# Spreading the dispatch of a soft mixture over its steps, and moving phi's fold and Mamba's weights into an expert stage

## The chip, the cores and the metric

The kernel runs on one core of one Trainium2 chip. The metric is device time in microseconds (us). Three runs of the kernel before took 2210.39, 2211.55 and 2219.65 us; the median is 2211.55.

## What is computed

Six residual layers over x of 4 x 1024 tokens of 128 features, in float32. Each layer reads a layer norm of x and adds its result to x. Cut to its core:

```python
x = x + 0.5 * moe(layernorm(x))       # "moe a": 8 experts, 2 of them for each token, hidden 512
x = x + mamba(layernorm(x))           # DI = 256, 16 states, convolution over 4 tokens
x = x + 0.5 * moe(layernorm(x))       # "moe b", the same weights
x = x + 0.5 * soft_moe(layernorm(x))  # "soft a": 64 experts x 32 slots
x = x + gla(layernorm(x))             # gated linear attention, 16 heads of 8
x = x + 0.5 * soft_moe(layernorm(x))  # "soft b", the same weights

def moe(x):        # cap = 1024 tokens for each expert
    top2 of softmax(x @ wg); a token takes the next free row of each of its two experts
    out = relu(rows @ w1[e] + b1[e]) @ w2[e] + b2[e]
    return gate0 * out[row0] + gate1 * out[row1]      # 0 where no row was free

def mamba(x):
    u, z = split(x @ W_in);  uc = silu(conv_b + conv4(u))
    dt, B, C = split(uc @ W_xproj);  delta = softplus(dt @ W_dt + b_dt)
    h[t] = exp(delta[t] * A) * h[t-1] + delta[t] * uc[t] * B[t]     # for 256 x 16 states
    return ((h . C + uc * D) * silu(z)) @ W_out

def soft_moe(x):
    logits = x @ phi_w.T + phi_b                       # (4096, 64 experts, 32 slots)
    rows = softmax(logits over slots).T @ x            # 2048 rows ("dispatch")
    y = tanh(layernorm(rows)) @ expert_w + expert_b
    return softmax(logits over experts) @ y            # "combine" of the soft layer
```

## The kernel before

**Layout.** x stays in on-chip memory as 32 tiles of 128 tokens (NT = 32). Nearly all work goes by groups of four tiles, 512 tokens. A layer norm of a group is: bn_stats and bn_aggr for each tile and "eps" (variance + 1e-5) on VectorE, one power of -0.5 on GpSimd (ln_pow), minus mean times that on VectorE (ln_minus), and then ScalarE applies scale and bias to a tile when it is needed (ln_apply, L201).

**Order.** In the main stretches (`with tc.manual_schedule(engines=ENGINES)`) TensorE, VectorE, ScalarE and GpSimd take their instructions in the order in which the program writes them. Each engine has one queue; an instruction waits for its data at the head of it, and all behind it wait too. Where nothing depends on it, SP's order, and the order outside these stretches, is the compiler's: an instruction may be put ahead of its place in the text as far as its data and its memory are free. Tiles come from pools: a pool that is opened in memory which another has held waits for the other's last reader.

**Stage by stage.** *Front* (L1821 and on): x is loaded, normed and routed. moe_routes makes constants on GpSimd (L212 to L235: a triangle, iotas, masks), once for moe a and once for moe b; `route.slots` turns the choice of experts into lists of rows. The expert weights are loaded here (w1, w2, b2) and y2_d, the place of moe a's results in device memory, is cleared.

*moe a* (moe_experts). 64 gathers of 128 tokens each (L417, an indirect DMA that GpSimd issues) bring rows of xn_d; 16 blocks of four are transposed (turn, L435 and L437), multiplied by w1 (hidden, L445) and w2 (output, L459, with the bias added on VectorE at L464); then 64 scatters (L423) put the rows into y2_d. In GpSimd's queue a scatter of block b - 1 follows each gather of block b + 4. The parameter `extra` takes a generator, of which one piece is run after each block; moe a has none, moe b has the loads of the soft layers' expert weights (arrive).

*Fold* (soft_weights, L943 to L979), after moe a: phi is loaded (1 MB), and for each of four stretches of 512 slots its squares are summed by a matmul and its last row is subtracted (a second matmul), so that 127 features carry the product and the 128th the bias; the largest norms give a flag, which is compared at L1870 to choose soft_bounded or an unbounded soft_layer. With the given inputs soft_bounded runs.

*Combine and Mamba's beginning* (combine L498 to L546, mamba_layer from L600). Groups of y2_d are loaded by SP (L508, two DMAs for each group, one for each of the token's two experts). A group's work: ScalarE scales the first expert's half by its gate, VectorE weighs the second half and adds x (four times L511), adds both (L526), takes statistics; then pow, minus. Mamba's own weights are loaded, cw (convolution weights times W_in, L638), A and dg are made. Then the first half sequence of 512 tokens passes `prologue` (L661 to L744): xn (L201), transposes, xT (L663), four projections pu (L682 and on), Silu, pp (L700), dbc, delta's matmuls, Abs and Relu, Exp, Ln, and on VectorE four instructions that end in du (L744). While it runs, three pieces of the groups 1 to 7 are put in after each of its steps (9 pieces for a group). Then come the states' scans (L805): 8 halves x 16 states; 10 of 16 states have their products on VectorE and 6 on GpSimd.

*moe b*, as moe a, but its results go with plain stores to ys_d, by expert and row (no scatter).

*soft a* (soft_bounded, L1035 and on). It takes moe b's results back itself (collect, L560 to L580): 64 gathers from ys_d by GpSimd (L560, tag "L", from a pool of 14 tiles), ScalarE's scale by the first gate, `add` on VectorE (four weighings L576 and one addition), statistics, root, minus. The main loop has one step k for each half tile: 64 steps in which TensorE makes logits (L1069), VectorE their minimum (L1073), ScalarE Exp, VectorE the sums over slots (total), GpSimd dm = ex * 1/sum (L1090, "weigh"), TensorE the dispatch matmuls (spread, three steps later). Eight steps are one group g; while it is at hand, step w = 0 adds the next group's results, 1 and 2 take its statistics, 4 and 5 norm it, 6 or 7 transposes it, and ScalarE scales the group after it at step 7. Logits have two buffers in PSUM. 12 gathers are issued ahead of the first scaling, 6 more behind it, then one in each step (18 + k). Before all that GpSimd sets rows 96 to 127 of xT to one (L1035).

After these 64 steps come the experts and the combine of the soft layer, then GLA and soft b, which has no gathers and no addition.

Of the kernel before, what the change touches and what calls it, by code (L numbers as in the profile page):

```python
# [9 lines left out]
F32 = mybir.dt.float32  # L10
# [61 lines left out]
def macaron_kernel(ctx: ExitStack, tc: tile.TileContext, a: dict, out: bass.AP):  # L72
# [328 lines left out]
    def moe_experts(w1, w2, b2, tag, xn_d, src, dest=None, ys_d=None, extra=None):  # L401


        with ExitStack() as s1:
# [66 lines left out]
            with tc.manual_schedule(engines=ENGINES):  # L471
                for c in range(AHEAD * 4):
                    gather(c)
                turn(0)
                turn(1)
                hidden(0)
                others = extra(psh, "ph") if extra else iter(())
                for blk in range(NBLK + 1):
                    if blk + 2 < NBLK:
                        turn(blk + 2)  # L480
                    if blk + 1 < NBLK:
                        hidden(blk + 1)
                    for i in range(4):
                        c = (blk + AHEAD) * 4 + i
                        if c < NSB:
                            gather(c)
                        elif blk > 0 and dest is not None:
                            nc.gpsimd.memset(spacer, 0.0)
                        if blk > 0 and dest is not None:
                            scatter((blk - 1) * 4 + i)  # L490
                    if blk < NBLK:
                        output(blk)
                        if dest is None:
                            c = blk * 4
                            nc.sync.dma_start(out=ys_v[:, c : c + 4, :], in_=eos[blk])
                    next(others, None)
# [50 lines left out]

    def collect(gate, ln, ys_d, place):
# [23 lines left out]
        def add(g):  # L572
            y = ys.pop(g)
            x4 = x[:, g * 4 : g * 4 + 4, :]
            for i in range(4):
                nc.vector.scalar_tensor_tensor(  # L576
                    y[:, 1, i, :], y[:, 1, i, :], gate[:, 1, g * 4 + i : g * 4 + i + 1],
                    x4[:, i, :], ALU.mult, ALU.add,
                )
            nc.vector.tensor_tensor(x4, y[:, 0, :, :], y[:, 1, :, :], ALU.add)  # L580

        def stats(g, i=None):
# [8 lines left out]
            gather=gather, scale=scale, add=add, stats=stats,  # L591
# [8 lines left out]
    def mamba_layer(ln, ln_next, first, route, rxp):  # L600
# [5 lines left out]
        with ExitStack() as s:  # L606
# [10 lines left out]
            w_in = load("w_in", [D, 2 * DI], wp)  # L617
            w_x = load("w_x", [P, NC, XO[2] + DS], wp)
            w_dt = load("w_dt", [DR, DI], wp)
            w_out = load("w_out", [P, NC, D], wp)  # L620
            cw = wp.tile([P, DC, DI], F32, name="cw")
            nc.scalar.dma_start(
                out=cw.rearrange("p k c -> p (k c)"), in_=a["conv_wT"].partition_broadcast(P)
            )

            for k in range(DC):
                nc.vector.tensor_tensor(cw[:, k, :], cw[:, k, :], w_in[:, :DI], ALU.mult)

            def col(name, c):
                i = COLS[name].start + c  # L630
                return cols[:, i : i + 1]

            A = wp.tile([P, NC * DS], F32, name="A")
            nc.scalar.activation(A, cols[:, COLS["A_log"]], AF.Exp)
            nc.vector.tensor_scalar(A, A, -1.0, None, ALU.mult)
            dg = wp.tile([P, NC, P], F32, name="dg")
            for c in range(NC):
                nc.vector.tensor_scalar(dg[:, c, :], ident, col("D", c), None, ALU.mult)  # L638
# [6 lines left out]
            def prologue(b, h, r, ps=ps, tag="mm"):  # L645
# [102 lines left out]
                yield  # L748

# [131 lines left out]
            with tc.manual_schedule(engines=ENGINES):  # L881
                bring, pieces = first
                for j in range(0, 16, 4):
                    bring(j, wk)
                run(pieces(0, wk))


                others = (_ for j in range(4, NT, 4) for _ in pieces(j, wk))
                for _ in prologue(*halves[0], rs[0], psa, "dA"):
                    for _ in range(3):  # L890
                        next(others, None)
# [39 lines left out]
    def soft_weights(pool):  # L931
# [3 lines left out]
        phiN = load("phiT", [D, NS], pool)  # L935
        pbc = pool.tile([P, NSC], F32, name="pbc")
        flag = pool.tile([1, 1], I32, name="flag")
        with (
            tc.tile_pool(name="fold", bufs=2) as wk,
            tc.tile_pool(name="foldp", bufs=2, space=PSUM) as ps,  # L940
        ):
            pb = wk.tile([NSC, P], F32, name="pb", bufs=1)
            nc.scalar.dma_start(out=pb, in_=a["phib"].rearrange("(c p) -> c p", p=P))  # L943
            ones = wk.tile([P, P], F32, name="ones", bufs=1)
            nc.gpsimd.memset(ones, 1.0)
            n2 = wk.tile([P, NS // 512], F32, name="n2", bufs=1)
            for q in range(NS // 512):
                qs = slice(q * 512, (q + 1) * 512)
                sq = wk.tile([P, 512], F32, name="sq")
                nc.scalar.activation(sq, phiN[:, qs], AF.Square)  # L950
                pn = ps.tile([P, 512], F32, name="pn")
                nc.tensor.matmul(pn, ones, sq, start=True, stop=True)
                nc.vector.tensor_reduce(n2[:, q : q + 1], pn, AX.X, ALU.max)
                pr = ps.tile([P, 512], F32, name="pr")
# [4 lines left out]
                nc.vector.tensor_tensor(phiN[:, qs], pr, phiN[:, qs], ALU.subtract)  # L959

            pt = ps.tile([P, 512], F32, name="pt", tag="pn")
            nc.tensor.transpose(pt[:, :NSC], pb, ident[:NSC, :NSC])
            nc.scalar.copy(pbc, pt[:, :NSC])
            ab = wk.tile([P, 1], F32, name="ab", bufs=1)
# [4 lines left out]
            pc = ps.tile([P, 512], F32, name="pc", tag="pr")  # L969
            nc.tensor.matmul(pc[:, 0:1], ones, ab, start=True, stop=True)  # L970
            nm = wk.tile([P, 1], F32, name="nm", bufs=1)
            nc.vector.tensor_reduce(nm, n2, AX.X, ALU.max)
            nc.vector.tensor_scalar(nm, nm, MAX_N2, None, ALU.is_le)
            nc.vector.tensor_tensor(nm, nm, pc[:, 0:1], ALU.add)
            nc.vector.tensor_scalar(flag, nm[0:1, :], float(P + 1), None, ALU.is_equal)
            nc.scalar.activation(pb, pb, AF.Copy, scale=-1.0)
# [3 lines left out]
        return phiN, pbc, flag  # L980
# [30 lines left out]
    def soft_bounded(phiN, phiM, pbc, ew, eb, tag, ln, first=None, rest=None, after=None, last=False):  # L1011
# [12 lines left out]
        with ExitStack() as s:  # L1024
# [10 lines left out]
            nc.gpsimd.memset(xT[96:P, :], 1.0)  # L1035
# [212 lines left out]
            with tc.manual_schedule(engines=ENGINES):  # L1248
                if first:
                    for n in range(12):  # L1250
                        first.gather(n, lp)
                    first.scale(0)
                    first.add(0)
                    first.stats(0)
                    first.root(0)
                    for n in range(12, 18):
                        first.gather(n, lp)
                    first.minus(0)
# [7 lines left out]
                for k in range(NK + CS * NB + XL + 3):  # L1266
# [7 lines left out]
                    if first and new:  # L1274
                        if w == 0:
                            first.add(g)
# [4 lines left out]
                        elif w == 4:  # L1281
                            first.minus(g)
                    if k < NK:
                        logits(k)
                        expo(k)
                        if first and new:
# [8 lines left out]
                            if r == 7 and 4 * (g + 1) < NT:  # L1295
# [23 lines left out]
                    if first and k < NK:  # L1319
                        if new and w == 2:  # L1320
                            first.root(g)
                        first.gather(18 + k, lp)
# [479 lines left out]
    with tc.tile_pool(name="moewa", bufs=1) as wpool:  # L1802
        with tc.tile_pool(name="rtmpa", bufs=1) as tp:
            route = moe_routes("a", tp)
            with (
# [13 lines left out]
                with tc.manual_schedule(engines=ENGINES | {mybir.EngineType.SP}):  # L1819
# [3 lines left out]
                    for j in range(0, NT + 32, 4):  # L1823
# [4 lines left out]
                        if j == NT + 8:  # L1828
                            weights = moe_weights(wpool)
                            clear()  # L1830
                        if j == NT + 8:
# [3 lines left out]
        moe_experts(*weights, "a", route.xn_d, src, dest)  # L1835

    spool = ctx.enter_context(tc.tile_pool(name="softw", bufs=1, side="right"))
    phiN, pbc, flag = soft_weights(spool)
    with tc.tile_pool(name="rtmpb", bufs=1, side="right") as tp:
        route = moe_routes("b", tp)  # L1840
        with tc.tile_pool(name="rxb", bufs=1) as rxp:
            mamba_layer(lns[1], lns[2], combine(gates[0], lns[1], 4, "hst"), route, rxp)
# [3 lines left out]


# [117 lines left out]
```

## Time and profile before

The profiled execution took 2220.05 us, and its span, from the first to the last instruction, is 2218.2 us. TensorE's clock was granted at 0.93 of its full speed in the mean.

| stretch, us from the span's start | work | TensorE busy | VectorE | ScalarE | GpSimd | granted clock |
|---|---|---|---|---|---|---|
| 0 to 65 | front, routes and slots a | 34.2 | 41.1 | 25.6 | 22.1 | 1.00 |
| 65 to 230 | moe a | 136.6 | 23.1 | 45.1 | 127.1 | 0.95 |
| 230 to 289 | fold, combine, Mamba's beginning | 27.0 | 41.3 | 32.1 | 10.7 | 0.64 |
| 289 to 815 | Mamba, routes b | 453.9 | 440.5 | 345.4 | 456.5 | 0.93 |
| 815 to 845 | slots b | 10.2 | 24.6 | 8.5 | 9.0 | 0.50 |
| 845 to 979 | moe b | 125.0 | 21.0 | 44.0 | 60.4 | 0.93 |
| 979 to 1519 | soft a | 486.5 | 370.1 | 189.1 | 352.4 | 0.97 |
| 1519 to 1710 | GLA | 164.9 | 139.8 | 83.2 | 78.6 | 0.79 |
| 1710 to 2218 | soft b | 481.1 | 312.5 | 178.9 | 277.2 | 0.98 |

Busy times are in us. "Busy" counts an instruction from its start to its end; instructions that issue DMAs count only for the issue, so a DMA's own time stands in a row of its queue ("SPq"), not of an engine. A row of the timeline reads: start, duration, engine, line, operation, output<-inputs, size, number of instructions drawn together, and in brackets the idle time of the engine before it and what ended that ("<-issue" where the profile shows nothing that it waited for).

### The profile page before, as it was taken

The numbers are of one execution on the slowest core, as the hardware profiler recorded it, in microseconds if no ns is written. First come the engines' busy times: TensorE is split into PE (matmuls) and PEld (weight loads), VectorE is DVE, ScalarE is ACT, GpSimd is POOL, SyncE is SP. The second block draws the span as 40 slices with busy tenths as digits, with TensorE's granted clock in tenths as the row PEclk, the third lists the DMA queues.
The fourth block names the chain that finished last, engine by engine and source line by source line (L and its number), as shares of the span: only waits on it lengthen the run. The fifth ranks groups of instructions, "written<-read, shape, count | busy, mean of one in ns | idle before, by whom it ended". The sixth has DMA issues, their size and how long they took to land. (4 is left out here: it accounts for less than half of the span.)

```text
span 2218.2 us, 17984 instructions
## 1 busy us (share of the span) xinstructions
PE 1919.3 (87%) x5893; PEld 888.6 (40%) x5893; DVE 1414.1 (64%) x1838; ACT 951.9 (43%) x1595; POOL 1393.9 (63%) x899
## 2 busy tenths in 40 slices
PE   5788578888989867968999899998887999989998
PEld 4556223333333324743333344442233444444443
DVE  6211678888888882128889555566876788744445
ACT  4322466677776623323333333333442333333331
POOL 3777278898988946526786566662434455556663
PEclk9999789999999877988999999998877999999999
DMA  7111432333333323420000000000000000000000
GB/s 255 44 52 52 148 104 96 108 117 101 125 106 99 116 95 81 122 59 20 18 17 9 1 1 0 1 0 6 0 0 1 1 0 0 1 1 5 10 10 16
DMA packets 65117, 110.70 MB, mean 50 GB/s; under 512 B 8159, under 2 KB 41583, under 8 KB 60149
## 3 DMA queue, kind: packets, MB, share of 16 engines
q1 hardware_dynamic: 53222, 85.04, 11.8%
q0 software_dynamic: 8192, 16.79, 2.9%
q10 hardware_dynamic: 3602, 7.65, 1.1%
q8 instruction: 48, 0.79, 0.2%
q14 instruction: 53, 0.43, 0.1%
HBM read 90.00 MB, written 19.44 MB: 49 GB/s over the span
## 5 line engine op out<-in xcount | busy, mean ns | idle before, releaser
L1090 POOL TENSOR_TENSOR dm<-ex,sm 128x1024 f32<-128x1024 f32 x128 | 245.8, 1921 | 174.1 <-DVE sm L1086 91.9
L822 POOL TENSOR_TENSOR hc<-hst,Cs 128x1024 f32<-128x1024 f32 x127 | 282.4, 2231 | 53.7 <-DVE hst L805 28.2
L1198 POOL TENSOR_TENSOR acc<-acc,L 128x1024 f32<-128x1024 f32 x96 | 225.8, 2352 | 117.0 <-ACT L L1190 116.3
L837 PE MATMUL py<-hc,ident 128*128 128x512 f32 x512 | 271.0, 658 | 24.3 <-POOL hc L822 24.1
L1190 ACT ACTIVATE L<-pl,pbc 128x512 f32<-128x512 f32 x256 | 161.9, 683 | 284.4 <-PE pl L1180 273.9
L1078 ACT ACTIVATE ex<-l,nmh 128x1024 f32<-128x1024 f32 x128 | 142.6, 1114 | 301.1 <-DVE nmh L1073 301.1
L1069 PE MATMUL l<-phiT,xT 128*128 128x512 f32 x512 | 247.5, 607 | 12.7 <-ACT ex L1078 9.2
L1101 PE MATMUL px<-dm,xn 128*128 128x512 f32 x512 | 244.1, 600 | 7.7 <-POOL dm L1090 7.7
L1180 PE MATMUL pl<-xT,phiM 128*128 128x512 f32 x512 | 245.3, 604 | 0.0
L1224 PE MATMUL py<-L,yt 128*128 128x512 f32 x512 | 238.5, 593 | 4.4 <-DVE L L1214 4.4
L1073 DVE TENSOR_REDUCE nmh<-l 128x1 f32<-128x1024 f32 x128 | 155.2, 1213 | 75.6 <-PE l L1069 75.6
L795 ACT ACTIVATE dA<-delta,A 128x512 f32<-128x512 f32 x256 | 177.0, 720 | 51.2 <-DVE hst L805 46.1
L787 POOL TENSOR_TENSOR dBu<-du,Bs 128x1024 f32<-128x1024 f32 x78 | 172.3, 2210 | 1.7 <-DVE du L744 1.2
L449 ACT ACTIVATE hT<-ph,cols 128x512 f32<-128x512 f32 x128 | 87.9, 687 | 192.0 <-PE ph L445 192.0
L805 DVE TENSOR_TENSOR_SCAN hst<-dA,carry,dBu 128x512 f32<-128x512 f32 x128 | 155.2, 1262 | 11.8 <-ACT dA L795 6.3
L837 PEld LDWEIGHTS py<-hc,ident 128*128 128x128 f32 x512 | 93.7, 197 | 167.8 <-issue 115.0
L805 DVE TENSOR_TENSOR_SCAN hst<-dA,dBu 128x512 f32<-128x512 f32 x128 | 147.4, 1202 | 16.9 <-POOL dBu L787 8.4
L1069 PEld LDWEIGHTS l<-phiT,xT 128*128 128x128 f32 x512 | 96.3, 193 | 147.9 <-issue 109.8
L1085 DVE TENSOR_REDUCE sm<-ex 128x32 f32<-128x1024 f32 x128 | 154.5, 1207 | 0.0
L464 DVE TENSOR_TENSOR eo<-po,b 128x512 f32<-128x512 f32 x32 | 22.1, 691 | 199.4 <-PE po L459 199.4
L1224 PEld LDWEIGHTS py<-L,yt 128*128 128x128 f32 x512 | 97.0, 190 | 127.1 <-issue 116.8
L1101 PEld LDWEIGHTS px<-dm,xn 128*128 128x128 f32 x512 | 95.1, 192 | 129.8 <-issue 102.8
(266 smaller groups left out, 3059.8 us busy)
## 6 DMA issues: line engine op xcount, KB each, us to landing
Cs<-bc_d SPq DMA_DIRECT2D x32, 1024.0 KB, 4.7
Bs<-bc_d SPq DMA_DIRECT2D x78, 256.0 KB, 3.3
w<-in_w SPq DMA_DIRECT2D x4, 2048.0 KB, 12.6
y_d<-zero SPq DMA_DIRECT2D x1, 4096.0 KB, 24.6
y<-y_d SPq DMA_DIRECT2D x16, 256.0 KB, 3.6
ys_d<-eo SPq DMA_DIRECT2D x16, 256.0 KB, 2.3
ew<-in_ew ACTq DMA_DIRECT2D x12, 320.0 KB, 3.9
x<-in_x SPq DMA_DIRECT2D x8, 256.0 KB, 7.9
```

The costliest lines, as they stand in the source:

```text
L787: eng.tensor_tensor(dBu, r["du"], r.pop(("B", n)).unsqueeze(2).to_broadcast([P, HB, NC]), ALU.mult,)
L795: nc.scalar.activation(dA, r["delta"][:, :, c], AF.Exp, scale=A[:, c * DS + n : c * DS + n + 1],)
L805: nc.vector.tensor_tensor_scan(hst[:, :, c], r.pop(("dA", n, c)), dBu[:, :, c], 0.0 if h == 0 else carry[b][:, c, n : n + 1], ALU.mult, AL ...
L822: eng.tensor_tensor(hc, r.pop(("h", n)), Cs.unsqueeze(2).to_broadcast([P, HB, NC]), ALU.mult)
L837: nc.tensor.matmul(r["py"][:, c, :], ident, hc[:, :, c], start=False, stop=(n == DS - 1))
L1069: nc.tensor.matmul(l[:, q * 512 : (q + 1) * 512], xT[:, j * P : (j + 1) * P], phiN[:, o : o + 512], start=True, stop=True,)
L1090: nc.gpsimd.tensor_tensor(dms[k], exs.pop(k), sms.pop(k).unsqueeze(2).to_broadcast([P, NG, PS]), ALU.mult,)
L1101: nc.tensor.matmul(px[hf * 2 + q], xns[j // 4][:, j % 4, :], dmf[:, q * 512 : (q + 1) * 512], start=(j == 0), stop=(j == NT - 1),)
L1180: nc.tensor.matmul(pl[:, i, :], phiM[:, (2 * c + i) * P : (2 * c + i + 1) * P], xT[:, t * TB : (t + 1) * TB], start=True, stop=True,)
L1190: nc.scalar.activation(L[:, i, :], pl[:, i, :], AF.Exp, bias=pbc[:, 2 * c + i : 2 * c + i + 1], scale=-1.0,)
L1198: nc.gpsimd.tensor_tensor(accs[t], accs[t], L, ALU.add)
L1224: nc.tensor.matmul(pys[t], yt[:, 2 * c + i, :], L[:, i, :], start=(c + i == 0), stop=(c == CS - 1 and i == 1),)
```

## The change

**Pools at the top.** The pools of phi (softw) and of Mamba's weights (mwts, new) are opened ahead of moe a on the right side of on-chip memory, and a pool for the fold's work beside them, which closes after moe a. Mamba's weights are released after Mamba. The pool of moe b's routing constants is opened after that, on the same side as before.

```diff
+    spool = ctx.enter_context(tc.tile_pool(name="softw", bufs=1, side="right"))
+    mpool = ctx.enter_context(ExitStack())
+    mwp = mpool.enter_context(tc.tile_pool(name="mwts", bufs=1, side="right"))
+    with (
+        tc.tile_pool(name="moewa", bufs=1) as wpool,
+        tc.tile_pool(name="fold", bufs=1, side="right") as fp,
+    ):
...
                             weights = moe_weights(wpool)
                             clear()
+                            phiN, pbc, flag, fold = soft_weights(spool)
+                            mweights, made = mamba_weights(mwp)
...
-        moe_experts(*weights, "a", route.xn_d, src, dest)
-
-    spool = ctx.enter_context(tc.tile_pool(name="softw", bufs=1, side="right"))
-    phiN, pbc, flag = soft_weights(spool)
+        def extra(ps, tag):
+            yield from fold(fp, ps, tag)
+            yield from made()
+
+        moe_experts(*weights, "a", route.xn_d, src, dest, extra=extra)
+
     with tc.tile_pool(name="rtmpb", bufs=1, side="right") as tp:
         route = moe_routes("b", tp)
...
-            mamba_layer(lns[1], lns[2], combine(gates[0], lns[1], 4, "hst"), route, rxp)
+            mamba_layer(mweights, lns[1], lns[2], lambda yp, tag: flow(gates[0], lns[1], yp, tag), route, rxp)
```

**Fold and weights as pieces.** phi and Mamba's weights are loaded by SP behind the expert weights and the clearing, instead of by ScalarE after moe a. The fold is a generator of six pieces (four stretches, two closing pieces) with the arithmetic of before; its ones are set by VectorE. mamba_weights gives two more pieces: cw, and A with dg. moe_experts runs these pieces after its blocks; the first two blocks run none, which holds for moe b's loads of expert weights too:

```diff
-                    next(others, None)
+                    if blk >= 2:
+                        next(others, None)
```

**Combine.** The new `flow` takes combine's place. A group is now two pieces; the first scales the next group and adds this one, the second holds minus of the group before it, statistics and pow:

```diff
+    def flow(gate, ln, yp, tag):
...
+        for j in range(0, 16, 4):
+            bring(j)
+        scale(0)
+        add(0)
+        ln_group(ln, 0)
+        yield
+        scale(4)
+        for j in range(4, NT, 4):
+            scale(j + 4)
+            add(j)
+            yield
+            if j > 4:
+                ln_minus(ln, j - 4)
+            ln_stats(ln, j)
+            ln_pow(ln, j)
+            yield
+        ln_minus(ln, NT - 4)
```

**Mamba's beginning.** The first half goes through a new `opening` instead of prologue: each tile's transpose follows its norm, Silu is applied to each projection as it comes out of PSUM (before: a copy or bias first, and Silu over both together), pp and dbc come after the third projection and ahead of the fourth, and delta's matmuls are not staggered. After each of its steps one piece of `flow` runs, after every second step two. The other seven halves go through prologue as before.

```diff
+            def opening(r, ps, tag):
...
+                        nc.scalar.activation(uc[:, q, :], pu, AF.Silu, bias=col("conv_b", q))
...
+                for q in range(NC + 1):
+                    project(q)
+                    yield
+                dbc = r["dbc"] = bp.tile([XO[2] + DS, HB], F32, name="dbc")
...
+                project(NC + 1)
+                yield
...
-                for _ in prologue(*halves[0], rs[0], psa, "dA"):
-                    for _ in range(3):
+                others = first(wk, "hst")
+                next(others)
+                for i, _ in enumerate(opening(rs[0], psa, "dA")):
+                    next(others, None)
+                    if i % 2:
                         next(others, None)
                 run(others)
```

**Dispatch of soft a.** `add` is cut into `second` (two of the four weighings) and `total` (the addition). From group 2 on the weighings stand at steps 6 and 7 of the group before, ahead of the logits' minimum, and the addition alone at step 0; ScalarE's scaling of the next group moves from step 7 to step 5. Group 1 keeps its whole addition at its w = 0, which is step 2. Two more gathers are issued in front, and each step's gather is two further on. The ones in xT are set by VectorE in soft a, by GpSimd in soft b.

```diff
-            nc.gpsimd.memset(xT[96:P, :], 1.0)
+            (nc.vector if first else nc.gpsimd).memset(xT[96:P, :], 1.0)
...
-                    for n in range(12, 18):
+                    for n in range(12, 20):
...
                         if w == 0:
-                            first.add(g)
+                            if g == 1:
+                                first.add(g)
+                            else:
+                                first.total(g)
...
+                    if first and r >= 6 and 4 * (g + 1) < NT:
+                        first.second(g + 1, 2 * (r - 6))
...
-                            if r == 7 and 4 * (g + 1) < NT:
+                            if r == 5 and 4 * (g + 1) < NT:
                                 first.scale(g + 1)
...
-                        first.gather(18 + k, lp)
+                        first.gather(20 + k, lp)
```

## The prediction

> **What bounds the kernel now.** The page's first part comes first: TensorE is busy for 87% of the span, so I looked for the stretches where it is not.
>
> ```profile
> PE 1919.3 (87%) x5893; PEld 888.6 (40%) x5893; DVE 1414.1 (64%) x1838; ACT 951.9 (43%) x1595; POOL 1393.9 (63%) x899
> ```
>
> The chain that ended last goes back only to 1709 us, so each earlier stage is read from its own timeline (start us, duration us, engine, line; in brackets the idle time before and what ended it). Three places are touched by the change.
>
> First, the first expert stage. GpSimd issues 64 gathers and 64 scatters, one pair per 2.565 us, without a gap beyond the 0.30 us between issues. TensorE needs 7.45 us for a block of four and GpSimd 10.26, so from the sixth block on TensorE waits for gathers. GpSimd's queue ends the stage.
>
> ```profile
> 172.67 0.97 POOL L417 DMA_INDIRECT g<-xn_da,src  x1 [0.30 <-issue]
> 173.94 0.99 POOL L423 DMA_INDIRECT y_d<-eo,dest  x1 [0.31 <-DVE dT L437]
> ```
>
> Second, from the last scatter to Mamba's first scan: 60 us in which no engine is full. The reader should follow one chain: last scatter, load of y, weighing, layer norm, xn, projection, pp, the activations, du, scan. Beside it VectorE adds eight groups, 5.06 us apart (251.33 to 256.38), because each waits for GpSimd's pow.
>
> ```profile
> 228.76 0.97 POOL L423 DMA_INDIRECT y_d<-eo,dest  x1 [0.19 <-issue]
> ...
> 231.03 2.59 SPq L508 DMA_DIRECT2D y<-y_d  x5
> ...
> 243.57 1.65 ACT L201 ACTIVATE xn<-x,nmr,rstd 128x128 f32<-128x128 f32 x4 [1.79 <-DVE nmr L145]
> ...
> 248.13 2.90 PE L682 MATMUL pu<-xT,cw 128*128 128x512 f32 x3 [2.37 <-ACT xT L663]
> ```
>
> ```profile
> 256.38 1.13 DVE L511 SCALAR_TENSOR_TENSOR y<-y,gate,x 128x128 f32<-128x128 f32 x4
> ...
> 262.88 3.70 PE L700 MATMUL pp<-uc,w_x 128*80 128x512 f32 x4 [4.22 <-ACT uc L693]
> ...
> 273.02 1.28 ACT L733 ACT_TABLE_LOAD   x1
> ...
> 286.17 1.25 DVE L744 TENSOR_TENSOR du<-delta,uc 128x1024 f32<-128x1024 f32 x1
> ...
> 288.85 2.34 DVE L805 TENSOR_TENSOR_SCAN hst<-dA,dBu 128x512 f32<-128x512 f32 x2
> ```
>
> Third, the first soft layer's dispatch. One group is eight logits steps. TensorE's own need is 8 x 3.43 + 0.44 (transposes) = 27.9 us. The logits of steps 8, 16 and 24 start at 1036.93, 1065.79 and 1097.31: group 2, whose addition fell into a wait of TensorE, took 28.86; group 3 took 31.5, and so did groups 4 to 7. In the second soft layer, without gathers and addition, it is 28.54 (1737.27 to 1765.81).
>
> ```profile
> 1065.79 1.88 PE L1069 MATMUL l<-phiT,xT 128*128 128x512 f32 x4
> ...
> 1066.93 2.76 DVE L576 SCALAR_TENSOR_TENSOR y<-y,gate,x 128x128 f32<-128x128 f32 x4
> 1067.16 2.06 POOL L1090 TENSOR_TENSOR dm<-ex,sm 128x1024 f32<-128x1024 f32 x1 [0.78 <-DVE sm L1086]
> ...
> 1091.28 1.23 DVE L1073 TENSOR_REDUCE nmh<-l 128x1 f32<-128x1024 f32 x1 [1.45 <-PE l L1069]
> ...
> 1095.79 1.23 DVE L1073 TENSOR_REDUCE nmh<-l 128x1 f32<-128x1024 f32 x1 [1.77 <-PE l L1069]
> ...
> 1097.31 1.88 PE L1069 MATMUL l<-phiT,xT 128*128 128x512 f32 x4
> ```
>
> The addition (2.76 + 0.69) stands ahead of step 0's minimum, so exp, and two steps later the logits, come late; at steps 6 and 7 VectorE is idle for 1.45 and 1.77.
>
> **Phi's fold and Mamba's weights into the expert stage: 0, but +2.1 on GpSimd.** TensorE gets 8 matmuls of 512 in two halves of 0.43, 1.72 a block for four blocks: 9.2 against GpSimd's 10.26, and the scatter of a block comes 6 to 10 us after its eo (eo of block 4 at 119.92, scatter at 132.9). VectorE gets 8 x 0.69, 4 x 0.42 and 2 x 0.47 with small ones, some 9.4 us in 160 of which it uses 22; ScalarE 4 x 0.63. The cover is GpSimd's queue; without it the fold would cost its 10 us. The loads (2 MB more behind w1, w2 and the clearing, which run at some 400 GB/s until 55) end near 60; the first gather is at 65.4. The load of phi no longer runs beside x at 1.7: at most 0.3 better, taken as 0.
>
> What moves with it is not in the diff. The second routing's constants lie in memory that the fold's pool now holds, so their GpSimd instructions (memsets, iotas, masks) fall from the first 10 us into the middle of the gathers: in the built program's order they stand behind gather 53 and ahead of scatter 33, at some 174 us.
>
> ```profile
> 7.17 0.20 POOL masks.py:65 MEMSET tri_f<- 128x128 f32 x1
> ...
> 9.11 0.12 POOL L232 MEMSET keep<- 128x8 f32 x1
> ```
>
> From 7.17 to 9.23 they take 2.06, free today (the front runs at VectorE's 3.09 a group). Behind them wait all later gathers and scatters: the last scatter comes 2.1 later (0.8, if they fill the 1.1 us gap at 209.6, to 3.4, if each issue behind them loses its 0.30 too). They don't wait for the fold, which ends near 155.
>
> **Mamba's beginning: -10.6, so -8.5 with the set-up.** The first y load is issued at 231.03 + 2.1 = 233.1 and its first half landed 3.4 later (234.36 today), the second at 237.0. Four weighings 1.22, addition 0.73, statistics 1.90: 240.9. Pow, minus, xn's start 1.36 (242.21 to 243.57 today): 242.2. Then xn 1.65, eight scalings 2 x 1.26 on the same engine, copy of xT 0.56: 247.0 (248.0 today). Projections 0 and 1 cost 5.4 + 3.4 as today, but Silu is put on each at once: pp at 256.8 (262.88), dbc at 260.3 (267.2), Exp's table load at 266.2, Ln done at 272.1. VectorE ends later. Group 4's addition waits for its scaling, its statistics end at 247.8; with minus put a group later a group costs 3.95 (1.22 + 0.73 + 1.90 + 0.1) instead of 5.06, six of them 23.7, 1.0 for a wait on scaling 16, 1.3 for the last minus: 273.9. Only then w, l, delta, du, 4 x 1.23, and dBu 1.25: first scan at 280.3 against 288.85. Bounds: -11 (landing at the fastest, VectorE not last) to -5 (groups at 4.5, y late). What follows is later one for one; Mamba's order is the same.
>
> **Expert weights from the third block on: 0.** Thirteen pieces now end with block 14; ew is first read at 1275. A piece lands in 3.9 us, the price if the last ys_d store had to share with it.
>
> **Ones by VectorE: -1.3.** Today GpSimd clears for 3.5 us, then gathers:
>
> ```profile
> 978.95 3.51 POOL L1035 MEMSET xT<- 32x4096 f32 x1 [51.10 <-PE po L459]
> 982.62 0.95 POOL L560 DMA_INDIRECT y<-ys_d,place  x1 [0.16 <-issue]
> ```
>
> The last ys_d store, issued at 978.8, lands at 981.2; gathers can start at 981.3. VectorE's memset is not in the trace: 1x512 took 0.48, so 4096 lie between 3.5 (GpSimd's) and 3.9; it has until 985. Bounds -1.3 to +1.0 (gathers wait for it).
>
> **Addition over three steps: -12.0, and +1.0 in group 1.** Step 0 keeps 0.69 of 3.45, which ends before the logits it waits for (end at 5.4 us of the step's count, addition at 5.4). The weighings go into the idle time at steps 6 and 7: at 6 behind a dm that ends at 1090.58, 0.5 more, before the minimum at 1091.28; at 7 beside a gather. Left on VectorE are statistics at steps 1 and 2 and eps, as in group 2. Its 28.86 is the nearest row; with 0.2 for the 0.69 I take 29.1, so 5 x (31.5 - 29.1) = 12.0 for groups 3 to 7. Bounds: 28.54 (14.8) and 30.5 (5.0). ScalarE's scalings at step 5 end before step 6's exp. In group 1, where TensorE waits for xn (1033), the pairs at steps 6 and 7 delay it by 1.0 (0 to 2.2). Two more gathers in front end at 1009.6, before the first dm at 1010.34.
>
> The row for a weighing is 0.25 to 2.58 us: three of four waited for dm. The Trainium skill (SBUF — State Buffer, Who interferes with whom) says that a VectorE instruction with two SBUF inputs contends with a GpSimd one that reads SBUF, and the first holds the ports to its end. This speaks against two pairs for one: by it each pair could wait for a whole dm, 2.45, an excess of 1.0 and 0.7 a group, and the sum would be 8.5 smaller. The trace agrees on the lock, but shows idle time there; I go by the rows.
>
> **Sum** against the profiled span of 2218.2 (2220.05 with what lies around it, 0.4% above the median of 2211.55): -8.5 - 1.3 - 12.0 + 1.0 = -20.8. The median becomes 2190.8. Bounds: -27 to -7.
>
> **Rivals.** (A) The dispatch stays tied: with GpSimd at 24.4 and VectorE at 27.2 of 31.5 us a group, one feeds the other late, and the period stays above 31. For: both would be near 90% full. Against: group 2 carried nearly the same. Then -8.5 - 0.3 - 1: 2202. (B) Mamba's beginning gains nothing, because y lands late or VectorE's groups keep 5.06: 7 x 1.1 more, with the set-up; then -12 + 0: 2199. (C) Slower: the lock between VectorE and GpSimd decides wherever VectorE got work: 9.4 in the expert stage hold the scatters one for one, the memset holds the first gathers (+1.0 for -1.3), the pairs take what the addition gave (12.0). -20.8 + 9.4 + 2.3 + 12.0 = +2.9: 2214. It decides once GpSimd's pair in the expert stage passes 2.565 by 0.15 for each pair. Against: some 30 copies and additions of 0.69 stand beside gathers today, and the pace held. (D) The first routing's constants too, or a pool that isn't free, make a wait on GpSimd at 174: each us is one us.
>
> **How the numbers follow.** Forecast 0.70, A 0.10, B 0.10, C 0.06, D and others 0.04. The predicted time is the forecast's, 2191, with 2184 to 2205 by its own bounds and some us for the runs' spread (2210 to 2220); the range 2180 to 2207 takes in A and B. A difference under 0.5% (11 us: 2200.5) can't be told from none. Faster: 0.68 of the forecast, 0.06 of B, 0.03 of A: 0.77; slower 0.06; the rest 0.17.
>
> **What would show it.** GpSimd's constants at 174 and a last scatter some 2 us later; first scan near 280; VectorE's groups 4 us apart; first gather at 981 less that shift; logits of steps 16 and 24 some 29.1 apart. I am wrong if the set-up waits, if du is not last on VectorE, or if the period stays at 31.5.

## The result, and the profile after

The changed kernel took 2190.12 us in the median of four runs (2189.43 to 2191.88), the kernel before 2210.97 (2207.62 to 2219.65): a ratio of 0.9905, with a 95% interval of 0.9883 to 0.9927. The forecast was 2191, in a range of 2180 to 2207.

TensorE is as busy as before in share, in a shorter span (the page's first part):

```profile
PE 1895.3 (87%) x5893; PEld 882.4 (40%) x5893; DVE 1408.3 (64%) x1840; ACT 949.5 (43%) x1593; POOL 1388.7 (63%) x897
```

The profiled execution is another matter: its span is 2188.8 against 2218.2 us, 29.4 less. The table follows the same events in both.

| event, us | before | changed | difference | by the prediction |
|---|---|---|---|---|
| last scatter of moe a issued | 228.76 | 231.94 | +3.2 | +2.1 |
| first xn of Mamba | 243.57 | 243.30 | -0.3 | -1.4 |
| first scan of Mamba | 288.85 | 279.82 | -9.0 | -8.5 |
| first gather of moe b | 844.83 | 837.26 | -7.6 | -8.5 |
| last eo of moe b | 978.07 | 970.46 | -7.6 | -8.5 |
| first gather of soft a | 982.62 | 974.54 | -8.1 | -9.8 |
| logits of step 8 | 1036.93 | 1030.27 | -6.7 | -8.8 |
| logits of step 16 | 1065.79 | 1060.16 | -5.6 | -8.8 |
| logits of step 56 | 1223.29 | 1206.27 | -17.0 | -20.8 |
| last addition of soft a | 1518.75 | 1501.38 | -17.4 | -20.8 |
| first minimum of soft b | 1722.90 | 1695.59 | -27.3 | -20.8 |

GLA, in which nothing was changed, is 9.9 us shorter. The reason stands in the windows of both kernels (stretch, its length, then busy us and instructions of TensorE, its weight loads, VectorE, ScalarE and GpSimd, then TensorE's granted clock, DMA share and GB/s); the stretch is the same part of GLA:

```profile
1570.00:1600.00 30.00, 26.70 (x89) 9.72 (x88) 21.94 (x29) 10.85 (x17) 12.82 (x6) 0.71 0.00 1
```

```profile
1553.00:1583.00 30.00, 25.98 (x104) 8.38 (x104) 28.51 (x43) 14.46 (x23) 15.92 (x8) 1.00 0.00 1
```

At 0.71 against 1.00, TensorE got through 89 matmuls against 104; over all of GLA the same 591 keep it busy for 173.6 us at 0.77 before and for 163.4 at 0.82 in the changed kernel. In the kernels run later GLA takes 190 to 198 us between the same two events, against 204.1 in this profile of before. So that execution looks unlucky (2220.05 us, where the median is 2210.97); a second profile of before isn't on record. Up to the end of soft a the change is worth 17.4 us. The median says 20.85; 3.4 us of that the two profiles can't place.

Now the stages. In moe a, GpSimd's own timeline of the changed kernel:

```profile
172.77 0.97 POOL L418 DMA_INDIRECT g<-xn_da,src  x1 [0.30 <-issue]
173.74 0.22 POOL masks.py:65 MEMSET tri_f<- 128x128 f32 x1
...
175.66 0.13 POOL L232 MEMSET keep<- 128x8 f32 x1
176.38 1.02 POOL L424 DMA_INDIRECT y_d<-eo,dest  x1 [0.59 <-issue]
```

The second routing's constants are where the prediction put them; the scatter behind them starts 2.64 us after the gather ahead of them has ended, where 0.30 is usual. Ahead of them the pace stays at 2.565 a pair (eight pairs from 112.37 to 132.89), behind them at 2.57 (eleven from 176.38 to 204.66). Later one scatter waits for its data, eo, as none does before:

```profile
223.03 0.97 POOL L424 DMA_INDIRECT y_d<-eo,dest  x1 [0.85 <-DVE eo L465]
```

So the delay against the kernel before is 0.10 us at the gather of 172.77, 2.44 at the scatter of 176.38, 2.51 at that of 221.09, and 3.18 from 223.03 on.

From the last scatter to the first scan (timeline of all engines; rows of eight instructions out of some two hundred):

```profile
231.94 0.96 POOL L424 DMA_INDIRECT y_d<-eo,dest  x1 [0.19 <-issue]
...
243.30 1.65 ACT L201 ACTIVATE xn<-x,nmr,rstd 128x128 f32<-128x128 f32 x4 [4.79 <-DVE nmr L145]
...
252.44 1.13 DVE L574 SCALAR_TENSOR_TENSOR y<-y,gate,x 128x128 f32<-128x128 f32 x4
...
256.19 1.13 DVE L574 SCALAR_TENSOR_TENSOR y<-y,gate,x 128x128 f32<-128x128 f32 x4
...
257.05 1.88 PE L866 MATMUL pp<-uc,w_x 128*80 128x512 f32 x4
...
270.41 1.06 ACT L898 ACTIVATE l<-w 128x1024 f32<-128x1024 f32 x1
...
273.37 1.22 DVE L900 SCALAR_TENSOR_TENSOR w<-w,e 128x1024 f32<-128x1024 f32 x1
...
279.82 2.34 DVE L963 TENSOR_TENSOR_SCAN hst<-dA,dBu 128x512 f32<-128x512 f32 x2
```

VectorE's groups are 3.75 apart (252.44, 256.19; one is 4.62) where they were 5.06. Ln ends at 271.47, and VectorE comes to w only at 273.37: it is last, by 1.9 us.

At the end of moe b, VectorE's ones and the first gather (the timeline again):

```profile
972.14 3.47 DVE L1193 MEMSET xT<- 32x4096 f32 x1 [0.99 <-DVE eo L465]
974.54 0.94 POOL L613 DMA_INDIRECT y<-ys_d,place  x1 [54.28 <-issue]
```

The gather no longer waits for GpSimd's clearing, and starts while VectorE is at it; it comes 3.4 us after the last eo has ended (971.15).

In the dispatch of soft a, group 3 (windows, from the logits of step 16 to those of step 24):

```profile
1060.16:1089.02 28.86, 28.43 (x69) 12.39 (x68) 25.82 (x40) 12.08 (x18) 24.53 (x18) 1.00 0.07 19
```

It is 28.86 us long instead of 31.5, and TensorE is busy for 28.43 of them. Step 22 of it, and then step 46 (timeline):

```profile
1081.90 0.89 DVE L629 SCALAR_TENSOR_TENSOR y<-y,gate,x 128x128 f32<-128x128 f32 x2
...
1082.46 0.99 POOL L613 DMA_INDIRECT y<-ys_d,place  x1 [0.16 <-DVE y L629]
...
1083.46 1.93 POOL L1248 TENSOR_TENSOR dm<-ex,sm 128x1024 f32<-128x1024 f32 x1
```

```profile
1166.94 3.80 POOL L1248 TENSOR_TENSOR dm<-ex,sm 128x1024 f32<-128x1024 f32 x2
...
1168.48 2.68 DVE L629 SCALAR_TENSOR_TENSOR y<-y,gate,x 128x128 f32<-128x128 f32 x2
...
1173.56 1.98 PE L1227 MATMUL l<-phiT,xT 128*128 128x512 f32 x4 [1.86 <-ACT ex L1236]
```

At step 22 a gather stands ahead of dm on GpSimd, and the pair of weighings goes first, in 0.89 us. The last gather is that of step 43, issued at 1165.94. At step 46 one dm follows the other at once, and the pair takes 2.68; exp is late, and the logits of step 47 wait 1.86 for it. That group, the sixth, takes 30.35; groups 3 to 5 take 28.86, group 2 29.89.

### The profile page after: what moved, and what is told of

Same layout as the page of the kernel before. It is cut to its first block, busy times and chain, and to the rows that moved or that the text cites. A ratio compares the mean times of both kernels' runs of the same rounds, so it can differ in the third digit from the quotient of the medians.

```text
span 2188.8 us, 17956 instructions
## 1 busy us (share of the span) xinstructions
PE 1895.3 (87%) x5893; PEld 882.4 (40%) x5893; DVE 1408.3 (64%) x1840; ACT 949.5 (43%) x1593; POOL 1388.7 (63%) x897
## 5 line engine op out<-in xcount | busy, mean ns | idle before, releaser
L995 PE MATMUL py<-hc,ident 128*128 128x512 f32 x512 | 273.6, 663 | 27.3 <-POOL hc L980 27.1
L1372 DVE TENSOR_TENSOR L<-L,rd 128x1024 f32<-128x1024 f32 x128 | 147.0, 1210 | 0.1
```

The costliest lines, as they stand in the source:

```text
L995: nc.tensor.matmul(r["py"][:, c, :], ident, hc[:, :, c], start=False, stop=(n == DS - 1))
```

## The experiments

Twelve runs follow, in four sets; each set has its own runs of the kernel before, since the chips differ. In the sets 1, 2 and 4 the kernel before takes 2254 to 2256 us, in set 3 2210. Most of the difference lies in the expert stages, where the chips of sets 1, 2 and 4 grant TensorE less clock. The changed kernel in set 2 and in the profile above, windows of moe a:

```profile
65.00:140.00 75.00, 53.99 (x237) 34.24 (x238) 10.33 (x16) 17.95 (x27) 49.29 (x51) 0.91 0.15 44
```

```profile
65.00:140.00 75.00, 65.37 (x320) 42.97 (x321) 15.47 (x24) 24.06 (x36) 56.98 (x59) 1.00 0.18 52
```

237 matmuls in 75 us against 320. The mean of 0.91 hides deep stretches: 0.51 from 115 to 125 us and 0.59 from 165 to 175, where the profile above has 1.00 and 0.98. There GpSimd waits for eo (up to 4.3 us at a time), with the next gathers behind it in its queue; TensorE sets the stage, and the last scatter comes at 255 to 261 in place of 230. So positions are compared within sets, or as distances inside one stage.

**The dispatch alone** (set 1): before, with the `second`, `total`, scaling and gather lines of the diff.

> The kernel before with the dispatch's edits alone: pairs of weighings at steps 6 and 7 from group 2 on, scaling at step 5, 20 gathers in front, each step's gather two further on. Fold, Mamba's beginning and the ones stay as before. Theory (the parts of the change act each for itself): the logits of steps 16, 24, 32 and 40 lie 28.9 us apart, steps 8 to 56 take 176.0 as in the changed kernel (186.4 before), and the start of group 1 costs 1.4; in all 9 us faster than before, some 2202. Rival (the addition is not what held the dispatch: GpSimd and VectorE set the period together, and the changed kernel's came from elsewhere): the period stays above 31 and the total within 2 us of before.

Measured: 2249.44, ratio 0.997 (0.9954 to 0.9986). Groups 3 to 5 take 28.87, and from the first gather to the minimum of step 56 it is 233.99 (233.65 in the changed kernel, 242.58 before). In the trace the 9 us are there (8.6 against the profile of before); the total shows 5.5, with 3 to 10 in its interval. The rival falls.

**All but the dispatch** (set 1): the changed kernel, those lines and the ones put back.

> The changed kernel with the dispatch and the ones as before (fold, Mamba's weights and beginning alone). Theory: last scatter at 231.9, first scan at 279.8 (before 288.85), of which 7.6 us are left at Mamba's last scan; periods of the dispatch 31.5; in all 7.6 us faster than before, some 2203. Rival (Mamba's beginning is given back later, as the other engines bound Mamba's stage): first scan at 279.8, but the last one within 3 us of before, and the total too.

Measured: 2243.51, ratio 0.9946 (0.9927 to 0.9965). First gather to step 56: 243.05, as before. From the last scatter to the first scan 49.4, against 59.96 in the kernel with the dispatch alone: -10.6. Where TensorE set moe a, the last scatter came at the same time in both (256.24 and 256.25), though only one has fold and constants there; so more was gained than the 7.6 expected. At the first scan it is 10.6 ahead, at the last 11.1: nothing is given back, and the rival falls.

**The old beginning with the fold in moe a** (set 1).

```diff
-                others = first(wk, "hst")
-                next(others)
-                for i, _ in enumerate(opening(rs[0], psa, "dA")):
+                bring, pieces = first
+                for j in range(0, 16, 4):
+                    bring(j, wk)
+                run(pieces(0, wk))
...
+                for _ in prologue(*halves[0], rs[0], psa, "dA"):
```

> The changed kernel, but the first half goes through combine's pieces and prologue as before; fold and Mamba's weights stay in the expert stage. Theory (two separate gains: the fold's work out of the wait between the last scatter and xn, 14.8 us before and 11.4 in the changed kernel, and the new order from xn to the first scan, 45.3 before and 36.5): xn at 243.3, first scan at 288.6, total 8.8 us above the changed kernel's, 2199. Rival (the fold out of the way lets VectorE's groups run at 4 us without the new order): first scan near 282, total some 2193.

Measured: 2243.05, ratio 0.9944 (0.9925 to 0.9963). From the last scatter to xn 11.24 (14.3 with the fold in between, 11.39 in the kernel without the dispatch); from xn to the first scan 45.13 (45.66 and 38.02). Two separate gains, 3.1 and 7.1 to 7.6 here; the rival, that the fold's absence would speed the groups, falls.

**The constants back at the start** (sets 1 and 2).

```diff
     mwp = mpool.enter_context(tc.tile_pool(name="mwts", bufs=1, side="right"))
+    bpool = ctx.enter_context(ExitStack())
+    btp = bpool.enter_context(tc.tile_pool(name="rtmpb", bufs=1, side="right"))
...
-    with tc.tile_pool(name="rtmpb", bufs=1, side="right") as tp:
-        route = moe_routes("b", tp)
+    route = moe_routes("b", btp)
```

> The changed kernel, but the pool of the second routing's constants is opened below the fold's, so that GpSimd makes them in the first 10 us as before the change. Theory (they lie on the path one for one, with the issues behind them): last scatter at 228.8 instead of 231.9, y's first load at 231.0, first scan at 276.6 instead of 279.8, total 3.2 us lower than the changed kernel's, 2187. Rival (the wait for y or VectorE's groups set the first scan, and the scatters had slack): last scatter at 228.8, but the first scan moves by less than 1.5, and the total too.

> The changed kernel with the second routing's constants back in the first 10 us. Theory: where GpSimd's queue sets moe a (pairs of gather and scatter 2.565 us apart), last scatter and first scan 3.2 us earlier than in the changed kernel, total 3.2 lower; where TensorE's clock sets it (the pairs further apart), no difference beyond 1 us. Rival: no difference in either.

Measured: ratios 0.9912 (0.9894 to 0.9931) and 0.9904 (0.9886 to 0.9923), no difference to the changed kernel's 0.9905 and 0.9899. Both ran where TensorE sets moe a, so that neither can tell. The last scatter even came later (260.1 and 258.3 against 254.9 to 258.1 in the five of these sets that keep the constants in moe a), and so it did in set 4 (260.6); why is open.

**The changed kernel again** (set 2).

> The changed kernel once more, beside the next three on the same chip. Theory (the gain belongs to the program, not to the chip that it was measured on): again 20 to 21 us below the kernel before; the dispatch's group that ends at step 48 takes 1.5 more than the others (step 46 to 47 in 5.9). Rival (a chip that grants less clock in the expert stages hides Mamba's set-up and gains more, or shows the fold): outside 15 to 26.

Measured: 2231.25 against 2256.01, ratio 0.9899 (0.988 to 0.9917): 24.8 less, more than the 20 to 21 expected but with them in its interval. Step 46 to 47 again in 5.9. But the group that ends at step 48 takes 32.06 us, 3.2 more than the others and not 1.5: step 47 to 48 takes 5.2 at a granted clock of 0.67, where it took 3.5 at 1.00. Two more kernels of sets 1 and 2 show the same (32.05 and 32.06); the other six with the long pair at step 46 have 30.4, as above.

**Pairs from group 3 on** (set 2): `if g <= 2: first.add(g)`, and `second` only from g = 2.

> The changed kernel, but the pairs of weighings begin with group 3; groups 1 and 2 are added whole as before. Theory (group 1's pairs delay the exps that TensorE waits for, and the wait that grows costs clock at step 8): from the first gather of soft a to the logits of step 16 some 83.2 us as before, not 85.6; total 2.4 below the changed kernel's. Rival (the pairs in group 1 lie in idle time and the clock falls anyway): 85 or more, total the same.

Measured: 2230.43, ratio 0.9905 (0.9871 to 0.994); the total can't tell it from the changed kernel. In the trace: first gather to the logits of step 16 83.3 us, against 84.8 in the changed kernel beside it and 85.6 in the one above. The theory holds for the stage, with 1.5 of the 2.4 expected beside its neighbour.

**18 gathers in front** (set 2).

```diff
-                    for n in range(12, 20):
+                    for n in range(12, 18):
...
-                        first.gather(20 + k, lp)
+                        first.gather(18 + k, lp)
```

> The changed kernel with 18 gathers in front and 18 + k in the steps, as before the change. In the changed kernel the last gather is at step 43; at steps 46 and 47 no gather stands ahead of dm, which starts with the sums, and the pair at step 46 took 2.68 us instead of 0.87. Theory (the gather ahead of dm is what lets the pair go first): with gathers up to step 45 the pair at step 46 takes under 1.0, the 5.9 us from step 46 to 47 become 4.4, total 1.5 lower. Rival (the further gathers in front are needed, or the long pair has another cause): 5.9 stays, or the scaling at step 5 waits for its gathers and the period grows above 29.

Measured: 2245.77, ratio 0.9941 (0.9917 to 0.9965): slower by 14.5 than the changed kernel beside it. 6.3 of it are in the dispatch (first gather to the minimum of step 56: 240.85 against 234.58); the rest is not where the edit is. Its timeline at steps 13 to 15:

```profile
1102.36 0.40 ACT L620 ACTIVATE y<-y,gate 128x128 f32<-128x128 f32 x1 [1.67 <-DMA y<-ys_d,place]
...
1105.42 0.60 DVE L629 SCALAR_TENSOR_TENSOR y<-y,gate,x 128x128 f32<-128x128 f32 x1 [2.14 <-DMA y<-ys_d,place]
```

The scaling waits for its last gather, with the next exp behind it on ScalarE, and the pair at step 7 waits with the minimum behind it on VectorE. The reason in the theory is confirmed: with a gather ahead of dm the pair at step 46 takes 0.89. Its gain isn't: step 46 to 47 takes 5.44, not 4.4, as the next pair now waits for its gather and takes 2.98. The rival's wait for gathers came true, with periods of 29.8 to 30.9.

**The last group later** (set 3): twelve of flow's pieces in the beginning, the rest one to a scan.

```diff
+                budget = iter(range(12))
...
-                run(others)
...
                     at(scan, k)
+                    next(others, None)
```

> The changed kernel, but combine's last two pieces and a bit (group 7 and the end of group 6) run between the first scans instead of ahead of du. In the changed kernel Ln ends 1.9 us before VectorE comes to w, l, delta and du. Theory (VectorE's groups set the first scan): from the last scatter to the first scan 46.0 to 46.3 us instead of 47.9 to 48.2. What is left of it at Mamba's last scan is open, as VectorE then has the group beside its scans. Rival (ScalarE's chain or GpSimd's pow ends last): no change.

Measured: 2186.27, ratio 0.9891 (0.9874 to 0.9908). From the last scatter to the first scan 47.1 instead of 47.9 (48.3 in the next kernel of this set, which has the old place of the last group). VectorE did set it, but ScalarE is close behind: now w waits for Ln, which itself comes at 272.2, 0.7 later than in the changed kernel.

```profile
272.22 1.23 DVE L900 SCALAR_TENSOR_TENSOR w<-w,e 128x1024 f32<-128x1024 f32 x1 [3.10 <-ACT l L898]
```

So 0.7 to 1.2 of the 1.9 came here; the kernel with three edits, below, has this edit too and shows 2.0. At the last scan it is 5.2 ahead of the changed kernel; see the clock below.

**Pairs behind the minimum** (set 3): the two lines of `second` moved below `logits(k)` and `expo(k)`.

> The changed kernel with the pairs of weighings behind the logits' minimum of steps 6 and 7 instead of ahead of it. Theory (a pair that stands ahead of the minimum delays exp and so TensorE where it waits, and at step 46, where no gather holds dm back, it waits for a whole dm): step 46 to 47 in 4.4 us instead of 5.9, first gather of soft a to the logits of step 16 in 83.5 or less instead of 84.8 to 85.6, the other groups 28.9 as before; in all 3 to 3.5 below the changed kernel's distance from the kernel before (ratio some 0.9886 where it has 0.990). Rival (behind the minimum the pair delays the sums, dm and the dispatch matmuls instead): step 46 to 47 above 5 or a group above 29.5.

Measured: 2191.13, ratio 0.9904 (0.9884 to 0.9924). Step 46 to 47 takes 4.40, as expected, but groups 3 to 6 take 29.8 each, as the rival said, and first gather to step 56 is 236.63, 3.0 more than in the changed kernel. From the first gather to the logits of step 16 it is 86.2, not the 83.5 expected. Its timeline at step 15:

```profile
1060.23 1.91 POOL L1248 TENSOR_TENSOR dm<-ex,sm 128x1024 f32<-128x1024 f32 x1 [0.99 <-DVE sm L1244]
...
1061.35 1.26 DVE L629 SCALAR_TENSOR_TENSOR y<-y,gate,x 128x128 f32<-128x128 f32 x2
```

Here the pairs of steps 14 to 39 fall into dm (1.73 us at step 14, 1.26 at step 15; 0.61 at steps 46 and 47), the sums behind them come late, and dm waits 0.99 for them, where it waits 0.02 at the same step of the changed kernel.

**Three edits together** (set 3): constants at the start, last group later, pairs behind the minimum.

> Three edits on the changed kernel together: the second routing's constants in the first 10 us, combine's last group between the first scans, the pairs behind the minimum. Theory: where GpSimd's queue sets moe a, 3.2 + up to 1.9 + 3.2 us below the changed kernel (8.3); where TensorE's clock sets moe a, the first is 0, and some 3 to 5 are left: ratio to the kernel before 0.987 to 0.9885. Rival (they don't add, since Mamba and the clock take back what comes early): 0.990 as in the changed kernel.

Measured: 2192.72, ratio 0.9921 (0.9907 to 0.9935), worse than theory and rival both. The last scatter is at 229.74, against 231.54 and 232.19 in the two kernels of its set that make the constants in moe a: 1.8 to 2.4 earlier. This is the only run of that edit where GpSimd sets the stage, and it shows the price of the constants. From there to the first scan it takes 46.3 us. The first scan, at 276.06, is 2.6 ahead of the kernel with the last group later; at the last scan nothing of that is left (780.78 and 780.84), and the pairs cost their 3.0.

**The edits that the traces spoke for** (set 4): constants at the start, last group later, pairs from group 3 on.

> The changed kernel with the three edits that the traces so far speak for: the second routing's constants in the first 10 us, combine's last group between the first scans, pairs of weighings (ahead of the minimum, as in the change) from group 3 on. Theory (where GpSimd's queue sets moe a): last scatter near 229.7, first scan near 276, first gather of soft a to the logits of step 16 in 83.3; in all 2.2 + 0.7 + 2.3 = 5.2 us below the changed kernel, ratio to the kernel before 0.988, if TensorE's clock gives nothing back. Rival (the clock's drops in Mamba's third and fourth halves, 67.8 + 66.1 us instead of 64.8 + 64.5, take the first two): ratio 0.9895 to 0.990.

Measured: 2237.95, ratio 0.9913 (0.989 to 0.9937). Its dispatch is the shortest of all (first gather to step 56: 231.36), but the last scatter came at 260.6, and Mamba's fifth and sixth halves took 67.6 and 66.0 us, 4.3 more than they mostly take, in a profile of the slowest of its six executions (2243.40). No version is shown to beat the changed kernel: the best ratio, 0.9891, lies well inside the intervals of 0.9905 and 0.9899.

## Why the prediction was right, point by point

*The set-up (+2.1) and the fold (0).* Together they are 3.2, near the upper bound that was given (3.4). The kernel with three edits keeps the fold, drops the constants, and ends 1.0 behind the kernel before: so the constants are worth some 2.2, near the 2.1 predicted; the changed kernel's own rows say 2.3 (2.64 - 0.30). The rest is not a fixed price of the fold. Up to the constants the delay is 0.10; 0.7 of it comes at one scatter, which waits 0.85 for an eo that TensorE brings late. Two other kernels with the fold show that wait (0.79 and 0.78), the one with the last group later doesn't. Why eo is late there wasn't isolated.

*Mamba's beginning (-10.6).* Measured from the last scatter to the first scan: 60.1 before, 47.9 after, -12.2. Fold and weights out of the way give 3.4 of it, the new order 8.8, and the old-beginning kernel shows that they are separate. Ln was to end at 272.1 and VectorE to follow at 273.9; it was 271.5 and 273.4. From xn to VectorE's w the forecast has 31.7, the trace 30.1: a group of VectorE costs 3.75, where 3.95 was taken. The first scan at 279.8, where 280.3 was forecast, is thus two misses that cancel, 1.1 in the set-up and 1.6 here, which is luck. That VectorE ends last is shown by the two kernels with the last group later in set 3; its margin of 1.9 is worth 0.7 to 2.0.

*"What follows is later one for one."* Wrong by 1.4 in this profile: of 9.0 at the first scan 7.6 are left at moe b. In other pairs of runs nothing was lost, or all of 2.6. Mamba's halves show where: from the second to the sixth most take 64.4 to 65.1 us, but some pair of them takes some 67.7 and 66.1: in nine of the fourteen profiles the third and fourth, in that of before the second and third, in one the fifth and sixth, in three none. In the changed kernel the third half has a stretch (472 to 488) with a granted clock of 0.68.

*The ones (-1.3).* Measured -0.5: from the last eo to the first gather 4.08 instead of 4.55, and the same two numbers (4.07 to 4.08, and 4.55) recur in all twelve runs by the engine that sets the ones. The step that failed is "gathers can start at 981.3", 2.5 us behind the store's issue. The first gather started 3.4 us behind it; what it waited for there the trace doesn't show.

*The addition over three steps (-12.0, +1.0 in group 1).* The period is 28.86 where 29.1 was taken. Groups 3 to 7 gain 2.66, 2.64, 2.65, 1.15 and 2.29, together 11.4. The rule of the Trainium skill that spoke against it (SBUF — State Buffer, section Who interferes with whom: a VectorE instruction with two SBUF inputs contends with a GpSimd instruction that reads SBUF, and the first holds the ports to its end) would have cost each group 1.7. (The 2.45 us there are a dm and a pair together; a dm alone takes 1.90 to 2.06 in that profile.) The trace shows it once, at step 46, with 1.8 us more for the pair and 1.5 for the group; where the clock falls behind it, as in the profile of the changed kernel in set 2, the group loses 3.2. In the others the gather ahead of dm lets VectorE go first; the prediction counted VectorE's idle time there, saw a gather at step 7, and didn't ask where the gathers end. Group 1's delay was 1.4. TensorE is busy for only 2.98 of the 5 us from 1020, and from 1025 to 1035 its granted clock is 0.55 and 0.77: another 1.0 in group 2, which no step had. In the profile of set 2 group 1 loses 1.75 and group 2 nothing.

*Two more gathers in front* were looked at only for their own end. They are what makes the pairs pay: without them 6 to 7 us of the dispatch are lost (240.85 from the first gather to step 56, where the kernel before takes 242.58).

*Rivals.* A (period above 31) and B (nothing from the beginning) didn't come. C's lock is real, and decided one pair of twelve. Of D nothing showed.

So the sum of -20.8 fits the median's -20.85 better than its terms deserve: by position they are -17.4 to the end of soft a. The places and the signs were right; that the sum agrees to 0.1 is luck.

## What to carry to other kernels

When an operation is put beside another engine's that shares its memory ports, look for what makes it go first (here a gather of 1 us), and follow that to the loop's end, where it may be missing. Where the reader of a load moves earlier in a schedule, the load must be counted against that reader, not only against its queue. And check a sum against positions, stage by stage: two profiles of the same code may lie 10 us apart in a stage that nobody touched.

## What the runs showed that was not expected

A GpSimd memset held up VectorE. In the kernel before, a copy of 128x128 (L1008), issued while GpSimd cleared xT (978.95 to 982.46), took 3.23 us; with the clearing on VectorE it took 0.22. In soft b, where GpSimd clears in all fourteen profiles, the same copy takes 2.74 to 3.02 and ends with the clearing.

```profile
979.31 3.23 DVE L1008 COPY smod<-sm 128x128 f32<-128x128 f32 x1
```

That agrees with the same section of the Trainium skill, by which a VectorE copy in its two-port mode and a GpSimd instruction shut each other out for the whole of one; that this copy ran in that mode no row shows. The prediction had counted the clearing's 3.5 us on GpSimd's queue alone.

Differences that go with TensorE's granted clock are larger than what most edits are worth: between chips 23 to 29 us at the last scatter of moe a, 10 us in GLA, 4 to 5 in Mamba's halves. What decides where it falls was not found.
